# Three dense passes of a graph network: row loads, chunk ends and the graph norm put in a fixed order

## The chip, the cores and the metric

The kernel runs on one core of a Trainium2 chip. The metric is the device time in microseconds (us) of one execution: the median of the kernel before is 2076.03 us over 15 runs (2070.28 to 2085.3). A core has five engines that run at the same time, each with its own queue of instructions: PE (TensorE, products), DVE (VectorE), ACT (ScalarE), POOL (GpSimd) and SP (SyncE, which here only issues DMAs). "PEld" is the load of weights into PE, listed apart.

## What is computed

Four layers over a graph of 6250 nodes with 128 features and 206,250 edges (100,000 pairs in both directions and one loop for each node). Each layer starts with a layer norm and a relu, and is added to its input. Cut to what matters for the change:

```python
# layer 1: mean over neighbours, then a norm over all nodes (one graph)
agg = segment_sum(h[src], dst) / max(deg, 1)
f = gelu(agg @ Wl.T + bl + h @ Wr.T)
out = f - mean_scale * f.mean(0)
x = x + out / sqrt((out * out).mean(0) + EPS) * gn_weight + gn_bias + h
# layer 2: mean over the "cliques" that a node points to (dst clipped to 3124)
x = x + (segment_sum(x_clique[clique], src) / max(count, 1)) @ W.T + b
# layer 3: a gated unit on the sum of messages
hh = relu(layernorm(x)) @ W_in.T + b_in
agg = segment_sum((hh @ W_msg)[src], dst)
r, z = sigmoid(...), sigmoid(...)          # of agg @ W_ih.T and hh @ W_hh.T
n = tanh(i_n + r * h_n)
x = x + ((1 - z) * n + z * hh) @ W_out.T + b_out
```

The sums over edges are taken as products with a matrix of counts: `cnt[s, d]` is the number of edges from node s to node d.

## The kernel before

Nodes are handled in blocks of 128: 49 blocks (`NB`). The first part of the program (to about 1130 us of the profiled execution) goes through the edges in strips, builds the count matrix with one-hot products, writes it to memory (`cnt_d`), writes its transpose for the first 25 blocks (`cntT_d`), and does layer 0 and the products of layer 1 that need no neighbours. It leaves in memory `h_d` (the input of layer 1's sum), `f_d` (the part of layer 1 without neighbours) and `u_d` (the running x). Most strips stand in `with tc.manual_schedule()`: there every engine issues its instructions in the order of the source. Elsewhere a scheduler of the compiler picks the order on each engine.

What follows are three dense passes, written as one generator, `dense` (L889). A pass goes through 13 chunks of destination blocks (`CHUNKS`: twelve of four blocks and, as the seventh, one of a single block), and for each chunk through all source blocks in steps:

- Passes 1 and 3 (`by_node`): 49 source blocks, 7 a step, so 7 steps a chunk. A step's rows are 896 KB, loaded by SP from `cnt_d` (L899).
- Pass 2: 25 blocks of cliques, 5 a step, so 5 steps a chunk. A step's rows are 640 KB from `cntT_d` (L904).

A step loads its rows into the tile `ring` (three buffers), casts them from bf16 to a 32-bit format, a part on DVE into `some` (L910; in pass 1 L917, which also sums the counts) and a part on ACT into `others` (L911, L920), two buffers each, and runs two products for each source block into `acc` (L922): the features are split into two parts (`halves`, L581 and L582) so that single-pass products keep their precision. That makes 14 products a step in passes 1 and 3, 10 in pass 2.

When a chunk's last step is done, its end is worked off: ACT copies `acc` to `wa` (L998, L1049, L1093), and then

- in pass 1: a product with `wl`, DVE adds (L1004), gelu on ACT (L1008), and POOL sums over nodes into `f_sum` (L981);
- after pass 1 the graph norm: a product sums over partitions (L990), DVE subtracts the centre from all blocks (L1031, 13 instructions), ACT squares (L1033), POOL sums, and from these comes `gain` (L1037 to L1040);
- in pass 2: a product with `wc` (L1053), the load of x from `u_d` (SP, L1056), POOL adds (L1057), DVE multiplies and adds (L1058 to L1064), a layer norm (`norm`: statistics on DVE, L555; four relus on ACT, L569), POOL adds `b_out` to x (L1070), the store to `x_d` (SP, L1071), transposes (L1074), a product with `W_in` (L1078), one with `W_msg` (L1082), and the split into the parts that pass 3 uses;
- in pass 3: the gates (L1098 to L1101), L1105 to L1116, a product with `W_out` (L1120), the load of x from `x_d` (SP, L1122), a DVE add (L1124) and the store to the output (SP, L1126).

All these loads and stores go through SP's one queue. In the source of the kernel before a chunk's end stands whole behind its last step, and the scheduler decides where its instructions fall among the steps of the following chunk. Before pass 1 the source loads all of `h_d` and splits it, and after the first chunk it loads `f_d`, the weights (on ACT's queue, L507 and L514), the inverse degrees and all of `x_clique`.

Of the kernel before, what the change touches and what calls it, by code (L numbers as in the profile page):

```python
# [9 lines left out]
F32 = mybir.dt.float32  # L10
I32 = mybir.dt.int32
BF16 = mybir.dt.bfloat16
# [474 lines left out]
def fast(ctx: ExitStack, tc: tile.TileContext, a: dict, out: bass.AP, flag: bass.AP):  # L487
# [62 lines left out]
    def norm(xs, hs, nb):  # L550
# [3 lines left out]
        for j in range(nb):  # L554
            nc.vector.bn_stats(stats[:, j, :], xs[:, j, :])  # L555
            nc.vector.bn_aggr(mv[:, j, :], stats[:, j, :])
        std = small.tile([P, CB], F32, name="f_std")
# [332 lines left out]
    def dense(parts, by_node, seen=None):  # L890

        last, step, dve = (NB, KB, 4) if by_node else (NQB, KQ, 3)
        for c, (g, nb) in enumerate(CHUNKS):
            w = nb * P
            acc = psum.tile([P, CB * P], F32, name="acc", bufs=2)
            for q in range(0, last, step):
                if by_node:
                    t = ring.tile([P, CB, KB, P], BF16, name="ring")
                    nc.sync.dma_start(t[:, :nb].rearrange("p b k n -> p b (k n)"),  # L899
                                      cnt_d[c, :, :nb, q * P : (q + KB) * P])  # L900
                    t = t[:, :nb].rearrange("p b k n -> p k b n")
                else:
                    t = ring.tile([P, KQ, CB, P], BF16, name="ring")
                    nc.sync.dma_start(t[:, :, :nb].rearrange("p k b n -> p k (b n)"),  # L904
                                      cntT_d[:, q : q + KQ, g * P : g * P + w])
                    t = t[:, :, :nb]
                some = wide.tile([P, 4, CB, P], F32R, name="some")
                others = wide.tile([P, 3, CB, P], F32R, name="others")
                if seen is None:
                    nc.vector.tensor_copy(some[:, :dve, :nb], t[:, :dve])  # L910
                    nc.scalar.copy(others[:, : step - dve, :nb], t[:, dve:])  # L911
                for i in range(step):
                    rhs = some[:, i, :nb] if i < dve else others[:, i - dve, :nb]
                    if seen is not None:
                        total = seen[:, c, q + i : q + i + 1]
                        if i < dve:
                            nc.vector.tensor_scalar(rhs, t[:, i], 1.0, None, op0=ALU.mult,  # L917
                                                    op1=ALU.add, accum_out=total)
                        else:
                            nc.scalar.activation(rhs, t[:, i], AF.Copy, accum_out=total)  # L920
                    for j in range(2):
                        nc.tensor.matmul(acc[:, :w], parts[:, q + i, j, :], rhs,  # L922
                                         start=q + i + j == 0, stop=q + i + j == last)
            yield g, nb, acc


    h_parts = late.tile([P, NB, 2, D], F32R, name="parts")
    fh = late.tile([P, NPAD], F32, name="fh")
    f = fh.rearrange("p (b f) -> p b f", f=D)
    for i, (g, nb) in enumerate(GROUPS):  # L930
        nc.sync.dma_start(f[:, g : g + nb, :], rows(h_d, g, nb))
        halves(nc.vector, [h_parts[:, g : g + nb, i, :] for i in range(2)], f[:, g : g + nb, :])
    deg2 = late.tile([P, NCH, NB], F32, name="deg2")
    layer1 = dense(h_parts, True, deg2)
    first = next(layer1)

    for g, nb in GROUPS:
        nc.sync.dma_start(f[:, g : g + nb, :], rows(f_d, g, nb))
    wl, wc, w_in = (weights(late, n) for n in ("WlT", "WcT", "W_inT"))
    w_msg, w_out = (weights(late, n) for n in ("W_msg", "W_outT"))  # L940
    w_ih, w_hh = weights(late, "W_ihT", D, 3 * D), weights(late, "W_hhT", D, 3 * D)
    b_in = weights(late, "b_in", D, 1)
    b_ih, b_hh = weights(late, "b_ih", D, 3), weights(late, "b_hh", D, 3)
    b_rz = late.tile([P, 2], F32, name="f_b_rz")
    nc.vector.tensor_add(b_rz, b_ih[:, :2], b_hh[:, :2])

    mean_scale, gn_weight, gn_bias, bc, b_out = (
        row_everywhere(late, n, a[n]) for n in ("mean_scale", "gn_weight", "gn_bias", "bc", "b_out"))
    b_res = late.tile([P, D], F32, name="f_b_res")
    nc.vector.tensor_add(b_res, gn_bias, bc)  # L950

    inv1 = late.tile([P, NS * SB], F32, name="inv1")
    with nc.allow_non_contiguous_dma(reason="one number for each node, once"):
        nc.sync.dma_start(inv1, deg_d.rearrange("s p w -> (s p w)").rearrange("(b p) -> p b", p=P))
    nc.vector.tensor_scalar(inv1, inv1, 1.0, None, op0=ALU.max)
    nc.vector.reciprocal(inv1, inv1)

    q_parts = late.tile([P, NQB, 2, D], F32R, name="q_parts")  # L960
    for g in range(0, NQB, GB):
        nb = min(GB, NQB - g)
        xq = work.tile([P, GB, D], F32, name="xq")
        n = min(NQ - g * P, nb * P)
        if n < nb * P:
            nc.sync.dma_start(xq[:, nb - 1, :], a["x_clique"][NQ - 1 :, :].to_broadcast([P, D]))
        if n >= P:
            nc.sync.dma_start(xq[:, : n // P, :], rows(a["x_clique"], g, n // P))
        if n % P:
            nc.sync.dma_start(xq[: n % P, nb - 1, :], a["x_clique"][NQ - n % P :, :])  # L970
        halves(nc.gpsimd, [q_parts[:, g : g + nb, i, :] for i in range(2)], xq[:, :nb, :])
    last_row = late.tile([P, 1], F32, name="last_row")
    with nc.allow_non_contiguous_dma(reason="one row, once"):
        nc.sync.dma_start(last_row, a["x_clique"][NQ - 1 :, :].rearrange("o f -> f o"))

# [16 lines left out]

    f_sum = late.tile([P, CB, D], F32, name="f_sum")
    nc.gpsimd.memset(f_sum, 0.0)
    for g, nb, acc in chain((first,), layer1):
        w = nb * P
        agg = work.tile([P, CB * P], F32, name="wa")
        nc.scalar.copy(agg[:, :w], acc[:, :w])  # L998
        pa = psum.tile([P, CB * D], F32, name="pA")
        for j in range(nb):  # L1000
            s = slice(j * D, (j + 1) * D)
            nc.tensor.matmul(pa[:, s], agg[:, s], wl, start=True, stop=True)
        for j in range(nb):
            nc.vector.scalar_tensor_tensor(f[:, g + j, :], pa[:, j * D : (j + 1) * D],  # L1004
                                           inv1[:, g + j : g + j + 1], f[:, g + j, :],
                                           op0=ALU.mult, op1=ALU.add)
        fg = flat(f[:, g : g + nb, :])
        nc.scalar.activation(fg, fg, AF.Gelu)  # L1008
        over_nodes(f_sum, f[:, g : g + nb, :], g, nb)
    p_sum = over_all(f_sum)  # L1010
    center = late.tile([P, D], F32, name="center")
    nc.vector.scalar_tensor_tensor(center, p_sum, 1.0 / N, mean_scale, op0=ALU.mult, op1=ALU.mult)
    last_rows = late.tile([P, P], F32, name="last_rows")
    nc.vector.tensor_copy(last_rows, last_row.to_broadcast([P, P]))
    p_last = psum.tile([P, D], F32, name="pS")
    nc.tensor.matmul(p_last, last_rows, wc, start=True, stop=True)
    last_out = late.tile([P, D], F32, name="last_out")
    nc.scalar.copy(last_out, p_last)
    inv2 = late.tile([P, NB], F32, name="inv2")
    by_source = deg2.rearrange("p d s -> p s d")  # L1020
    nc.vector.tensor_reduce(inv2, by_source, axis=mybir.AxisListType.X, op=ALU.add)
    nc.vector.tensor_scalar(inv2, inv2, 1.0, None, op0=ALU.max)
    nc.vector.reciprocal(inv2, inv2)
    to_last = late.tile([P, NB], F32, name="to_last")
    nc.vector.tensor_reduce(to_last, by_source[:, :, -(-NQB // CB) :], axis=mybir.AxisListType.X, op=ALU.add)
    nc.vector.tensor_mul(to_last, to_last, inv2)

    sq_sum = late.tile([P, CB, D], F32, name="f_sum")
    nc.gpsimd.memset(sq_sum, 0.0)
    for g, nb in GROUPS:  # L1030
        nc.vector.tensor_sub(f[:, g : g + nb, :], f[:, g : g + nb, :], bcast(center, nb))  # L1031
        sq = work.tile([P, GB, D], F32, name="wb")
        nc.scalar.activation(sq[:, :nb, :], f[:, g : g + nb, :], AF.Square)  # L1033
        over_nodes(sq_sum, sq, g, nb)
    p_sq = over_all(sq_sum)
# [9 lines left out]
    for g, nb, acc in dense(q_parts, False):  # L1045
# [22 lines left out]
        for _ in norm(xg, h, nb):  # L1068
            pass
# [120 lines left out]
```

## Time and profile before

| What | us |
|---|---|
| Median of 15 runs | 2076.03 |
| The profiled execution, its own time | 2085.92 |
| Its span, from the first to the last instruction | 2083.9 |
| First product of pass 1 | 1137.1 |
| `wa` copies of pass 1, first, second, last | 1171.5, 1213.7, 1463.0 |
| `wa` copies of pass 2, first and last | 1498.6, 1699.2 |
| `wa` copies of pass 3, first and last | 1725.2, 2068.7 |

The page of the profile gives PE as busy for 90% of the span, DVE 66%, ACT 56% and POOL 22%; the mean granted clock of PE is 0.966 of full speed. The busy share of PE is a mean over stages, so the stages are looked at one by one: the views used below are the busy time of each engine in a window of time, the timeline (start, length, engine, line, operation, tiles, and in brackets how long the engine was idle before and who released it), the waits of an engine (who waited for whom, us in total, times, longest), and the chain of work that ended last. A time such as 1961.05 is in us from the start of the span.

### The profile page before, as it was taken

How to read it: one execution, taken by the hardware profiler on the slowest of the kernel's cores; microseconds unless marked ns; L12 is line 12 of the kernel's file. 1: busy time of each engine (PE TensorE's matmuls, PEld its weight loads, DVE VectorE, ACT ScalarE, POOL GpSimd, SP SyncE). 2: the span in 40 equal slices, each digit the busy share in tenths (PEclk: the TensorE clock that was granted, in tenths of full speed). 3: DMA queues.
4: the chain of work that ended last, by engine and by line, in shares of the span. 5: the costliest groups of instructions: out<-in, count | busy, mean ns of one | idle time of the engine just before them, and what ended most of it. 6: DMA issues, size and time to landing. Idle time of an engine off the chain costs nothing. (4 is left out here: it accounts for less than half of the span.)

```text
span 2083.9 us, 60004 instructions
## 1 busy us (share of the span) xinstructions
PE 1885.4 (90%) x25624; PEld 1539.7 (74%) x25624; DVE 1385.0 (66%) x2957; ACT 1174.7 (56%) x2717; POOL 462.5 (22%) x377
## 2 busy tenths in 40 slices
PE   1699999999999999999997599999699899999998
PEld 0677888888888788888876488888567677778775
DVE  5777787777777777777763587687765564433443
ACT  2866666666666666666661366566454554443443
POOL 3124333343234333343221200000421110000000
PEclk9799999999999999999998799999898999997999
DMA  2466777667867677677635998788476777766773
GB/s 59 125 150 185 178 196 181 182 178 192 187 161 191 182 195 178 181 179 192 165 84 187 245 295 259 232 285 271 123 235 186 224 248 238 237 192 220 237 237 125
DMA packets 423783, 406.29 MB, mean 195 GB/s; under 512 B 191216, under 2 KB 414307, under 8 KB 417235
## 3 DMA queue, kind: packets, MB, share of 16 engines
q1 hardware_dynamic: 414883, 394.35, 66.5%
q0 software_dynamic: 5600, 6.56, 1.2%
q8 instruction: 203, 3.33, 0.7%
q10 hardware_dynamic: 3024, 1.45, 0.4%
q14 instruction: 73, 0.60, 0.1%
HBM read 227.26 MB, written 134.89 MB: 174 GB/s over the span
## 5 line engine op out<-in xcount | busy, mean ns | idle before, releaser
L741 ACT CAST cnt<-pK 128x392 bf16<-128x392 f32 x784 | 405.7, 518 | 303.8 <-PE pK L736 256.1
L766 PE MATMUL pL<-edge_w,h 128*128 128x256 f32 (+1 forms) x2450 | 564.2, 381 | 0.3 <-ACT agg L770 0.3
L766 PEld LDWEIGHTS pL<-edge_w,h 128*128 128x128 f32 x2450 | 447.1, 192 | 56.0 <-ACT agg L770 0.5
L736 PEld LDWEIGHTS <-s_hot 64*128 64x128 bf16 x18816 | 361.8, 96 | 151.6 <-issue 111.7
L736 PE MATMUL pK<-k_hot,s_hot 64*128 64x49 bf16 (+1 forms) x18816 | 404.2, 194 | 68.0 <-ACT edge_w L741 24.4
L741 ACT COPY edge_w<-pK 128x392 f32<-128x392 f32 x784 | 414.5, 529 | 0.0
L922 PE MATMUL acc<-some,parts 128*128 128x512 f32 (+1 forms) x1456 | 374.0, 399 | 32.1 <-DVE some L917 22.0
L922 PEld LDWEIGHTS acc<-some,parts 128*128 128x128 f32 x1456 | 273.7, 196 | 97.2 <-DVE some L917 27.4
L911 ACT CAST others<-ring 128x1536 fp32r<-128x1536 bf16 (+3 forms) x156 | 192.4, 1233 | 203.4 <-PE acc L922 143.8
L715 DVE TENSOR_TENSOR s_hot<-iota,keys 128x2048 bf16<-128x2048 bf16 x196 | 239.1, 1220 | 89.6 <-ACT keys L697 55.1
L910 DVE CAST some<-ring 128x2048 fp32r<-128x2048 bf16 (+3 forms) x156 | 167.2, 1072 | 181.5 <-PE acc L922 171.6
L922 PE MATMUL acc<-others,parts 128*128 128x512 f32 (+1 forms) x1092 | 279.0, 390 | 0.0
L718 DVE TENSOR_TENSOR k_hot<-k_hot,by_edge 128x2352 bf16<-128x2352 bf16 x196 | 272.4, 1390 | 8.0
L917 DVE TENSOR_SCALAR_CACHE_REDUCE some<-ring 128x512 fp32r<-128x512 bf16 (+1 forms) x364 | 216.1, 651 | 66.7 <-DMA ring<-cnt_d 31.8
L922 PEld LDWEIGHTS acc<-others,parts 128*128 128x128 f32 x1092 | 204.5, 194 | 41.7 <-issue 0.5
L920 ACT ACTIVATE others<-ring 128x512 fp32r<-128x512 bf16 (+1 forms) x273 | 162.3, 597 | 112.9 <-issue 47.0
L625 POOL DMA_INDIRECT dst<-in_dst,off_i x50 | 82.4, 1649 | 403.8 <-DVE off_i L659 219.9
L922 PE MATMUL acc<-some,q_parts 128*128 128x512 f32 (+1 forms) x390 | 113.4, 418 | 31.2 <-DVE some L910 31.2
L717 DVE TENSOR_TENSOR k_hot<-iota,keys 128x784 bf16<-128x784 bf16 x196 | 113.5, 579 | 0.0
L922 PEld LDWEIGHTS acc<-some,q_parts 128*128 128x128 f32 x390 | 73.0, 201 | 51.9 <-DVE some L910 36.2
L625 POOL DMA_INDIRECT line<-in_dst,at_i x25 | 40.7, 1627 | 221.3 <-DVE at_i L638 218.7
L922 PE MATMUL acc<-others,q_parts 128*128 128x512 f32 (+1 forms) x260 | 80.3, 419 | 0.0
(158 smaller groups left out, 1571.2 us busy)
## 6 DMA issues: line engine op xcount, KB each, us to landing
ring<-cnt_d SPq DMA_DIRECT2D x168, 896.0 KB
cnt_d<-cnt SPq DMA_DIRECT2D x49, 1568.0 KB
cntT_d<-tt SPq DMA_DIRECT2D x175, 224.0 KB
ring<-cntT_d SPq DMA_DIRECT2D x60, 640.0 KB
ring<-cnt_d SPq DMA_DIRECT2D x14, 224.0 KB
xs<-in_x SPq DMA_DIRECT2D x12, 256.0 KB
xs<-in_x SPq DMA_DIRECT2D x24, 128.0 KB
u_d<-xs SPq DMA_DIRECT2D x24, 128.0 KB
```

The source lines that it names most:

```text
L625: nc.gpsimd.indirect_dma_start(out=t, out_offset=None, in_=col[name], in_offset=bass.IndirectOffsetOnAxis(ap=idx, axis=0))
L715: nc.vector.tensor_tensor(s_hot, count_up(P), at(0, P), op=ALU.is_equal)
L717: nc.vector.tensor_tensor(k_hot[:, :, 0], count_up(NB), at(1, NB), op=ALU.is_equal)
L718: nc.vector.tensor_tensor(k_hot[:, :, 1:], k_hot[:, :, :1].to_broadcast([P, tq, 3, NB, TI]), parts.to_broadcast([P, tq, 3, NB, TI]), op=AL ...
L736: nc.tensor.matmul(pk[:, h, to], s_hot[r, u, :, t], rhs, start=j == 0, stop=True, skip_group_check=True)
L741: nc.scalar.copy(m.rearrange("p b (i h) -> p b i h", h=WN), by_block[:, i])
L766: nc.tensor.matmul(pl[:, :w], h0[:, s, :], edge_w[:, s, :w], start=s == 0, stop=s == NB - 1)
L910: nc.vector.tensor_copy(some[:, :dve, :nb], t[:, :dve])
L911: nc.scalar.copy(others[:, : step - dve, :nb], t[:, dve:])
L917: nc.vector.tensor_scalar(rhs, t[:, i], 1.0, None, op0=ALU.mult, op1=ALU.add, accum_out=total)
L920: nc.scalar.activation(rhs, t[:, i], AF.Copy, accum_out=total)
L922: nc.tensor.matmul(acc[:, :w], parts[:, q + i, j, :], rhs, start=q + i + j == 0, stop=q + i + j == last)
```

## The change

The three passes and the graph norm are put in one `with tc.manual_schedule()`, and the source itself now gives the order. `dense` loads and casts a step's rows (`bring`) one step ahead of its products, and yields after each step. A chunk's end is a generator too, cut by `yield` into pieces; after each step `between` moves every end that is running by one piece, and lets at most three run at once:

```python
        for n, (c, g, nb, q) in enumerate(steps):
            now = ready
            if n + 1 < len(steps):
                ready = bring(*steps[n + 1])
            if q == 0:
                acc = psum.tile([P, CB * P], F32, name="acc", bufs=2)
            for i in range(step):
                for j in range(2):
                    nc.tensor.matmul(acc[:, : nb * P], parts[:, q + i, j, :], now[i],
                                     start=q + i + j == 0, stop=q + i + j == last)
            yield (g, nb, acc) if q + step == last else None

    running, waiting = [], []

    def between(free=True):

        running[:] = [work for work in running if next(work, work) is not work]
        if free and waiting and len(running) < 3:
            running.append(waiting.pop(0))

    def run(layer, end, chores=()):

        chores = iter(chores)
        for done in layer:
            between()
            for chore in next(chores, ()):
                chore()
            if done:
                work = end(*done)
                next(work)
                waiting.append(work)
```

The first piece of an end is the copy of `acc`. Pass 1's end has two more, pass 2's eleven, pass 3's five. These are the pieces of pass 2's and pass 3's ends that hold the stores:

```python
        for _ in steps:
            pass
        nc.gpsimd.tensor_tensor(xg, xg, bcast(b_out, nb), op=ALU.add)
        nc.sync.dma_start(rows(x_d, g, nb), xg)
        yield
...
        yield
        po = psum.tile([P, CB * D], F32, name="pA", bufs=2)
        for j in range(nb):
            o = po[:, j * D : (j + 1) * D]
            nc.tensor.matmul(o, new[:, j * P : (j + 1) * P], w_out, start=True, stop=True)
        xg = flat(x[:, :nb, :])
        nc.vector.tensor_add(xg, xg, po[:, :w])
        if g + nb < NB:
            nc.sync.dma_start(rows(out, g, nb), x[:, :nb, :])
```

(The loop over `steps` is the rest of `norm`: DVE's reciprocal and shift, and the four relus.) The graph norm is a generator of thirteen pieces that runs beside the first thirteen steps of pass 2, two groups of four blocks to a piece; until it is through, pass 2's ends wait:

```python
        for i, (g, nb) in enumerate(GROUPS):
            nc.vector.tensor_sub(f[:, g : g + nb, :], f[:, g : g + nb, :], bcast(center, nb))
            sq = work.tile([P, GB, D], F32, name="wb", bufs=3)
            nc.scalar.activation(sq[:, :nb, :], f[:, g : g + nb, :], AF.Square)
            over_nodes(sq_sum, sq, g, nb)
            if i % 2:
                yield
...
        layer2 = dense(q_parts, False)
        next(layer2)
        normed = running[-1]
        for done in layer2:
            between(normed not in running)
            if done:
                work_2 = end2(*done)
                next(work_2)
                waiting.append(work_2)
        layer3 = dense(m_parts, True)
        next(layer3)

        def rest():
            while running or waiting:
                between()

        while waiting or len(running) > 2:
            between()
        run(layer3, end3, [[]] * 4 + [[rest]])
        rest()
```

The other edits: `h_d` is loaded and split group by group within the first chunk of pass 1, as its steps come to need it; the loads of `f_d`, `x_clique`, the weights and the rows of biases become "chores" put behind single steps of pass 1, a few to a chunk, and all go through SP; `m_parts` takes the place of `h_parts` in the same tile, `sq_sum` gets a tile of its own; `wa` has five buffers instead of two, `x` and `wb` three instead of two, `xq` one instead of two, and in PSUM `pA` has two and there is a new tile `pM`; the layer norm's statistics can be cut in two (a `yield 2` in `norm`). The products and the numbers that are computed stay the same.

## The prediction

> **What bounds the kernel now.** I read the busy time by stage first, cut where the ACT copies of a finished chunk (`wa<-acc`, lines 998, 1049, 1093) begin. The columns are the window, its length, the busy us (and instructions) of PE, PEld, DVE, ACT and POOL, the granted clock, the DMA share and GB/s:
>
> ```profile
> 1171.50:1213.60 42.10, 27.73 (x107) 20.57 (x108) 22.09 (x71) 18.10 (x51) 9.37 (x11) 0.80 0.92 255
> 1213.60:1463.00 249.40, 247.79 (x1162) 205.00 (x1161) 194.02 (x656) 153.59 (x479) 13.40 (x11) 0.99 0.82 265
> 1463.00:1498.60 35.60, 18.38 (x77) 14.28 (x77) 26.35 (x25) 15.70 (x24) 22.67 (x16) 0.72 0.36 107
> 1498.60:1699.20 200.60, 183.15 (x850) 140.99 (x850) 123.00 (x326) 104.96 (x166) 32.47 (x23) 0.96 0.70 213
> 1699.20:2068.70 369.50, 368.04 (x1531) 279.14 (x1530) 156.60 (x185) 159.68 (x148) 1.31 (x1) 0.97 0.69 224
> ```
>
> The dense passes run from 1137 (first `acc` matmul) to the end. Pass 1 is the first two rows: its second chunk takes 42.1 us, the others 23.4, PE full. Row 3 is the graph norm: PE idle for 17.2 us and on a low clock. Row 4 is pass 2: 17.4 us idle. Row 5 is pass 3: 1.5 us idle in 369.5. So what this change can win lies in pass 1's second chunk, the graph norm and pass 2; pass 3 has only its one-block chunk to win, and everything to lose.
>
> Second, the waits of SP, the queue that issues every row load of the passes:
>
> ```profile
> SPq L1126 <- DVE x L1124: 83.6, 12, 9.2
> ...
> SPq L1071 <- POOL x L1070: 37.9, 13, 5.1
> ```
>
> SP stands still before each store of a chunk until its data is ready; whatever is queued behind the store waits as well. Third, the timeline of pass 3 around one such store:
>
> ```profile
> 1961.05 1.13 PE L1120 MATMUL pA<-f_W_outT,wd 128*128 128x128 f32 x8
> ...
> 1962.22 0.69 DVE L1124 TENSOR_TENSOR x<-x,pA 128x512 f32<-128x512 f32 x1 [0.18 <-PE pA L1120]
> ...
> 1962.93 0.38 SPq L1126 DMA_DIRECT2D out<-x  x1
> 1964.23 0.54 SPq L899 DMA_DIRECT2D ring<-cnt_d  x1
> ```
>
> The output products end, DVE adds, SP stores at once, and the next row load waits only for its ring slot: the ACT cast before it ended at 1964.21. In this kernel the load follows as soon as a slot is free, so the store costs nothing. Fourth, what a row load takes when SP issues it late, at the start of pass 3 (two issues in one entry, at 1689.57 and 1690.50):
>
> ```profile
> 1689.57 1.47 SPq L899 DMA_DIRECT2D ring<-cnt_d  x2
> ...
> 1694.52 1.23 DVE L910 CAST some<-ring 128x2048 fp32r<-128x2048 bf16 x1 [2.31 <-DMA ring<-cnt_d]
> ...
> 1698.71 1.23 DVE L910 CAST some<-ring 128x2048 fp32r<-128x2048 bf16 x1 [2.96 <-DMA ring<-cnt_d]
> ```
>
> 896 KB land 4.95 us after issue, and the second load 3.3 us (4.19 less the 0.93 between issues) behind that.
>
> **The change, part by part.** In the changed source the order on SP is: rows of step n+1, then the DMAs of the end-pieces put after step n, then rows of step n+2. `E` is the end of step n's 14 matmuls.
>
> *Output stores in pass 3.* The last piece of a chunk's end (four products, add, store) is put after step 5 of the next chunk. The products run from E to E+1.05 (eight records, 1.06 at 1961 by the chain), the add ends 0.2+0.69 later, the store is issued at E+1.95 and takes 0.38: the rows of step n+2 go out at E+2.35. They land at E+7.3, the cast takes 1.23 (row above), PE can start step n+2 at E+8.6. Meanwhile it has only step n+1 to run, 14 matmuls in 3.2 us (86 in 19.70 us by the chain): done at E+4.25. Stall 4.3 us. I add 0.4, since the rows after these land 3.3 us later and a step is 3.2: 4.7. Eleven stores have rows behind them (the last one's steps are all loaded), one of them beside the short steps of the one-block chunk (1.6 more): 53 us. Bounds: a landing of 6.7 us (issue 1185.37, cast 1192.09) gives 72; a landing that is hidden gives 0. I take 4.95, since nothing else then fills the queue.
>
> *Stores of x_d in pass 2.* The piece with the relus comes after step n. ACT does the casts of step n+1 first, then:
>
> ```profile
> 1673.46 1.65 ACT L569 ACTIVATE wb<-x,f_shift,f_rstd 128x128 f32<-128x128 f32 x4 [0.44 <-DVE f_shift L565]
> 1675.18 1.28 POOL L1070 TENSOR_TENSOR x<-x,f_b_out 128x512 f32<-128x512 f32 x1 [8.07 <-ACT wb L569]
> ...
> 1676.48 0.36 SPq L1071 DMA_DIRECT2D x_d<-x  x1
> ```
>
> From relu to store is 3.0 us. ACT's casts (1.05) can't start before step n-1 frees `others`; counted from that, the store is at 1.25+3.0 = 4.3, the rows of n+2 at 4.75. 640 KB scaled from 896 KB (1.4 fixed, as 256 KB in 2.3 of the chain's `x_d<-x` leave after 0.9 at 285 GB/s, and 2.5 for the bytes) land 4.0 later, the cast takes 0.96: 9.7. PE has steps n and n+1 (10 matmuls, 2.29 each) and about 1.0 of pieces: 5.6 to 6.0. Stall 3.7, 4.7 if DVE is behind; I take 4.2. Counting the yields, the graph norm holds the ends back for 13 steps; then stores fall after steps 20, 21, 22, 31, 32, 37, 42, 47, 52, 57, 62. A store that follows another by one step finds no cover: 5.8. So 8 x 4.2 + 3 x 5.8 = 51 us, bounds 0 and 70.
>
> *What goes in pass 2:* the 17.4 us idle and the low clock (0.96 of 200.6 us, 8 us), 25 in all, if the pieces, a step apart, no longer make PE wait. Net +26.
>
> *Graph norm between steps.* Gone: 17.2 us idle and 4 us at half clock. New: seven steps with two subtractions each. In the trace 13 of them take 18.25 us on DVE beside POOL, 1.40 each, so 2 x 1.40 + 0.96 of cast = 3.76 a step against 2.29 of matmuls: 10.3 lost. Net -11, bounds -21 and 0.
>
> *Pass 1.* The second chunk goes from 42.1 to about 26: the loads of f, x_clique and the weights no longer stand in front of its rows. The first stays: h and rows, 9.6 MB at 258 to 285 GB/s, are 34 to 37 us, as now (34.5). The moved loads, 5.7 MB, come back in the steady chunks, at 265 GB/s now and 285 then, near the 316 GB/s of the fastest slice. Net -16, bounds -19 and 0. Its DVE waits (products, four adds of 0.34, then casts) fit in a step; if not, 0.2 a chunk.
>
> *From pass 2 to pass 3.* The last end is flushed after step 4 with nothing beside it (relu, transposes, copy, W_in, copy, W_msg, split: 8.2 us to PE's release, 2.4 of it PE work): 6. One pass 2 store holds rows of pass 3: 4. Products moved over: 3. The one-block chunk takes 28.1 us now, with a 6.3 us chain of gates and half clock; 6.5 of end products and the 14.0 it takes in pass 1 make 20.5, and the chunk after it gains 1.5: 9 back. Net +4.
>
> Sum: -16 - 11 + 26 + 53 + 4 = **+56**. The profiled execution took 2085.92 (span 2083.9), 9.9 above the median 2076.03 of 15; I add the difference to the median: **2132**.
>
> **Rules weighed.** The Trainium skill, "DMA: Bandwidth & Descriptors", section "Anatomy of one DMA — SWDGE (gpsimd) path", says that waits are served on the issuing sequencer before dispatch, which speaks against this order as SP's rows above do. Its fit for that path, 2.0 us plus bytes over 436 GB/s, would make the landing 4.1, an estimate, and the sum some 9 us smaller; the row's 4.95 decides. "TensorE: Matmul & The Clock Gate", Part 1, has the clock halve after an idle window of about 3.4 us, which my stalls exceed; by it each could cost up to 1.7 us more, an estimate.
>
> **Rivals.**
> 1. *The rows arrive in time* (SP's order is not the source's, or waits resolve earlier than I count), so both store terms vanish: -16 - 11 - 25 + 0 + 0 = -52, and rival DVE waits give some back: about **2028**. It decides where a store is issued 3 us before E. For it: three ring slots, and SP waits 83.6 us now without harm. Against: the strips already run in a fixed order, and there SP waits 164.5 us for its stores of `cnt` with transposes behind them.
> 2. *Stalls half as long*, since pieces of other chunks cover them: 56 - 52 = +4, **2080**.
> 3. *The clock falls after stalls.* After 2.3 us idle at 1671.8 the slice to 1680 has 0.91, 1.8 us lost; after 6.2 us near 1877 the next slice has 0.50. 22 stalls x 1.8 = 40 more: **2172**.
>
> **Numbers.** Forecast 0.62 (2105 to 2160), rival 3 0.13 (to 2190), rival 2 0.07 (2060 to 2105), rival 1 0.18. The range, 2060 to 2190, leaves out rival 1. 0.2% (4 us) is about what a measurement here can tell from no change: faster 0.22 (rival 1 and half of 2), same 0.03, slower 0.75.
>
> **What would show it.** Right: in pass 3 one PE gap of 4 to 5 us per chunk, before step 0, with the cast waiting for a row load that SP issued right after `out<-x`; chunks of some 33.6 us where they were 28.9; the same after `x_d<-x` in pass 2; no 42 us chunk in pass 1; no 14.7 us gap in the graph norm. Wrong: pass 3 still at 28.9 us per chunk, or casts that wait for something other than rows.

## The result, and the profile after

The changed kernel takes 2173.96 us (median of 9 runs, 2167.82 to 2176.8), the kernel before 2076.96 (47 runs): a ratio of 1.0461, 95% interval 1.0445 to 1.0477. It is slower by 97 us, where the forecast said 56 (2132, range 2060 to 2190). The profiled execution has a span of 2167.4 us and a mean granted clock of 0.957, where the one of before has 2083.9 and 0.966.

The first view of the changed kernel is again the busy time by stage, cut at the `wa<-acc` copies (now L1048). The rows are the second chunk of pass 1, pass 2 with the graph norm beside it, and pass 3; columns as before (window, length, busy us and instructions of PE, PEld, DVE, ACT and POOL, granted clock, DMA share, GB/s):

```profile
1169.90:1193.20 23.30, 23.30 (x107) 19.27 (x106) 19.08 (x63) 15.86 (x45) 1.29 (x1) 1.00 0.94 322
1442.50:1712.80 270.30, 209.27 (x903) 165.09 (x901) 157.75 (x349) 113.29 (x180) 54.91 (x39) 0.87 0.55 171
1712.80:2150.10 437.30, 381.19 (x1552) 287.60 (x1552) 158.15 (x191) 164.72 (x159) 2.56 (x2) 0.94 0.55 191
```

The second chunk of pass 1 takes 23.3 us where it took 42.1, and PE is never idle in it. Pass 2 takes 270.3 (before, 35.6 + 200.6 = 236.2) and pass 3 takes 437.3 (before, 369.5); in both PE now waits, at a lower clock and with the DMA engines half busy. By stage the change is -20.9 (pass 1: from the first product at 1137.5 to 1442.5), +34.1, +67.8 and +2.1 (what follows the last copy), together 83, the difference of the two spans.

The waits of SP, before the stores of the output and of `x_d`:

```profile
SPq L1201 <- DVE x L1199: 154.3, 12, 13.5
SPq L1138 <- POOL x L1137: 153.3, 13, 17.1
```

SP stands 308 us before these stores, where it stood 121.5 before the change. What stands behind shows in the timeline of a chunk of pass 3 (an entry that covers several issues, such as `x5`, gives the start of the first):

```profile
2001.80 2.00 PE L936 MATMUL acc<-some,parts 128*128 128x512 f32 x8
...
2006.10 0.69 DVE L1199 TENSOR_TENSOR x<-x,pA 128x512 f32<-128x512 f32 x1 [4.24 <-PE pA L1197]
2006.82 0.40 SPq L1201 DMA_DIRECT2D out<-x  x1
2007.30 9.74 SPq L902 DMA_DIRECT2D ring<-cnt_d  x5
...
2012.52 1.23 DVE L913 CAST some<-ring 128x2048 fp32r<-128x2048 bf16 x1 [5.74 <-DMA ring<-cnt_d]
...
2013.81 3.59 PE L936 MATMUL acc<-some,parts 128*128 128x512 f32 x8 [4.52 <-DVE some L913]
```

This is the forecast's sequence, item by item: DVE's addition behind the output products, SP's store as soon as it is done, the next rows 0.48 us later, the cast 5.2 after that, and PE idle for 4.52. One thing is new: the eight products behind the gap take 3.59 us, and eight such products take 2.00 us in a step without a gap (the first line). The same in pass 2, after the store of `x_d`:

```profile
1679.33 1.56 PE L936 MATMUL acc<-some,q_parts 128*128 128x512 f32 x6
...
1680.57 0.36 SPq L1138 DMA_DIRECT2D x_d<-x  x1
...
1681.09 5.92 SPq L907 DMA_DIRECT2D ring<-cntT_d  x4
...
1685.58 0.96 DVE L913 CAST some<-ring 128x1536 fp32r<-128x1536 bf16 x1 [6.76 <-DMA ring<-cntT_d]
...
1686.59 2.93 PE L936 MATMUL acc<-some,q_parts 128*128 128x512 f32 x6 [4.34 <-DVE some L913]
```

PE is idle for 4.34 us, and then six products take 2.93 us where six took 1.56 in the step before (the first line).

### The profile page after: what moved, and what is told of

Same layout as the page of the kernel before. It is cut to its first block, busy times and chain, and to the rows that moved or that the text cites. A ratio compares the mean times of both kernels' runs of the same rounds, so it can differ in the third digit from the quotient of the medians.

```text
span 2167.4 us, 60053 instructions
## 1 busy us (share of the span) xinstructions
PE 1902.9 (88%) x25624; PEld 1557.8 (72%) x25624; DVE 1390.4 (64%) x2957; ACT 1171.8 (54%) x2717; POOL 459.3 (21%) x377
## 5 line engine op out<-in xcount | busy, mean ns | idle before, releaser
L936 PE MATMUL acc<-some,parts 128*128 128x512 f32 (+1 forms) x1456 | 384.8, 409 | 71.3 <-DVE some L913 54.2
L936 PE MATMUL acc<-some,q_parts 128*128 128x512 f32 (+1 forms) x390 | 117.8, 443 | 60.2 <-DVE some L913 60.2
L936 PEld LDWEIGHTS acc<-some,q_parts 128*128 128x128 f32 x390 | 77.8, 214 | 84.7 <-DVE some L913 66.7
L627 POOL DMA_INDIRECT src<-in_src,off_i x50 | 75.9, 1517 | 15.4 <-issue 14.9
```

What stands on the lines that cost most here:

```text
L627: nc.gpsimd.indirect_dma_start(out=t, out_offset=None, in_=col[name], in_offset=bass.IndirectOffsetOnAxis(ap=idx, axis=0))
L936: nc.tensor.matmul(acc[:, : nb * P], parts[:, q + i, j, :], now[i], start=q + i + j == 0, stop=q + i + j == last)
```

## The experiments

The theory: row loads stand behind a store that waits on SP's queue; they land too late for the one step of cover that they have; and after the gap the products run slow. Its rivals: the pieces of the ends on PE, ACT and DVE cost the time, whichever queue the stores are on (A); the bytes of the stores beside the rows do (B); the clock is low for other reasons (C).

The runs are compared from the first product of the passes to the end of the span, "the passes", since the part ahead of them, which no edit touches, is not always equally long: it ends at 1136 to 1143 us in most profiles, but at 1188 to 1195 in e1 to e3 and e6, beside which the kernel before took 2135.68 us. The lengths, in us, cut at the same copies, are each read from one profiled execution; two executions of the changed kernel differ by 7 us in the passes, two of the kernel with both stores on POOL by 1:

| Kernel | time | ratio to before, 95% interval | pass 1 | pass 2 | pass 3 | end | the passes |
|---|---|---|---|---|---|---|---|
| before | 2076.96 | | 325.9 | 236.2 | 369.5 | 15.2 | 946.8 |
| changed | 2173.96 | 1.0461 (1.0445 to 1.0477) | 305.0 | 270.3 | 437.4 | 17.3 | 1030 |
| after_again | 2176.39 | 1.0470 (1.0436 to 1.0503) | 307.7 | 268.4 | 444.1 | 17.3 | 1037 |
| e1_out_2later | 2166.39 | 1.0147 (1.0098 to 1.0196) | 307.7 | 272.6 | 369.5 | 18.0 | 968 |
| e2_xd_2later | 2163.52 | 1.0135 (1.0080 to 1.0189) | 306.3 | 205.7 | 438.1 | 17.1 | 967 |
| e3_both_2later | 2087.83 | 0.9781 (0.9741 to 0.9821) | 306.6 | 209.1 | 364.8 | 18.1 | 899 |
| e6_pool_stores | 2086.75 | 0.9779 (0.9738 to 0.9819) | 307.9 | 204.7 | 359.3 | 20.1 | 892 |
| e4_both_1later | 2083.53 | 1.0017 (1.0001 to 1.0033) | 306.7 | 222.8 | 388.4 | 18.0 | 936 |
| e5_rows_3ahead | 2056.34 | 0.9883 (0.9857 to 0.9909) | 317.1 | 224.2 | 362.0 | 18.0 | 921 |
| e7_fill_gap | 2163.77 | 1.0401 (1.0373 to 1.0429) | 307.5 | 269.4 | 423.0 | 19.3 | 1019 |
| e6_again | 2029.34 | 0.9738 (0.9708 to 0.9769) | 306.5 | 204.2 | 359.2 | 21.4 | 891 |
| e8_pool_onegroup | 2028.89 | 0.9731 (0.9707 to 0.9755) | 307.8 | 197.7 | 359.2 | 21.5 | 886 |
| e9_act_out | 2027.93 | 0.9729 (0.9696 to 0.9761) | 307.4 | 203.2 | 359.5 | 17.8 | 888 |
| e10_pool_ahead3_onegroup | 2046.71 | 0.9813 (0.9787 to 0.9838) | 315.8 | 205.8 | 360.5 | 21.3 | 903 |

e1 to e3 and e6 were measured together, then after_again, e4, e5 and e7, both groups on a chip that the record numbers 15, and the last four together on chip 9. Why the part ahead took some 50 us more in the first group is not known. Every edit is one of the changed kernel, except where another is named.

**Each store two steps later, alone and together.** e1 moves the output store, e2 the store of `x_d`, e3 both.

```diff
         nc.vector.tensor_add(xg, xg, po[:, :w])
+        yield
+        yield
         if g + nb < NB:
             nc.sync.dma_start(rows(out, g, nb), x[:, :nb, :])
```

```diff
         nc.gpsimd.tensor_tensor(xg, xg, bcast(b_out, nb), op=ALU.add)
-        nc.sync.dma_start(rows(x_d, g, nb), xg)
         yield
...
         yield
+        nc.sync.dma_start(rows(x_d, g, nb), xg)
         ph = psum.tile([P, CB * P], F32, name="pB")
```

> The store of a chunk's output comes two steps later in the source; nothing else changes. Theory (rows stand behind the store on SP's queue, and their landing of some 5 us, the cast and the half clock after the gap are paid once a chunk): two steps later the output is long ready, SP does not wait there, pass 3 goes from 35 us a chunk back to about 29, its 437 us to about 370, passes 1 and 2 stay; about 2110 us, between 2100 and 2120. Rival A (the cost of pass 3 is PE's end pieces and DVE's adds in front of its casts, whichever queue the store is on): no change, 2174. Rival B (it is the store's bytes beside the rows): no change either, the gap only moves two steps.

> The store of x to x_d in pass 2 comes two pieces later in the source (ahead of the W_in product); nothing else changes. Theory (SP's queue): the eleven stalls of pass 2 go, 20.8 us a chunk back to about 16.5, pass 2 from 270 to some 215 us; pass 3 stays at 437; about 2120 us, between 2105 and 2135. Rival A (pieces on PE, ACT and DVE in the program's order): pass 2 stays near 270, 2174. Rival C (the clock, low for other reasons): gaps go but the granted clock of pass 2 stays near 0.87 and half of the gain is missing, about 2147.

> Both stores two steps later. Theory: the gains of the two alone add up, since they lie in different passes: pass 2 about 215 us, pass 3 about 370, some 120 us less than the changed kernel: 2050 us, between 2040 and 2065, and so below the kernel before (2077). Rival A or B: near 2174. If the half clock after gaps was a cost of its own, the mean granted clock rises from 0.957 to 0.97 or more.

The passes fall from 1030 us by 62 with e1, by 63 with e2 and by 131 with e3, near the sum of the two, and each edit changes its own pass alone: e1 takes pass 3 from 437.4 to 369.5 and leaves pass 2, e2 takes pass 2 from 270.3 to 205.7, further than the 215 expected, and leaves pass 3. (The whole times that the expectations give were missed by 38 to 56 us, since they counted on the shorter part ahead of the passes; the stages are what can be compared.) Rivals A and B, which expected no change, are out. Rival C is too: the granted clock of e2's pass 2 is 0.98 where it was 0.87, so it was low because of the gaps.

**The same places, another queue.** e6 leaves the stores where the change put them in the source, and issues them on POOL's queue.

```diff
-        nc.sync.dma_start(rows(x_d, g, nb), xg)
+        nc.gpsimd.dma_start(rows(x_d, g, nb), xg)
...
-            nc.sync.dma_start(rows(out, g, nb), x[:, :nb, :])
+            nc.gpsimd.dma_start(rows(out, g, nb), x[:, :nb, :])
```

> Both stores keep their place in the source but are issued on POOL's queue, so that no row load stands behind them; their bytes and times are the same. Theory (the order on SP's queue): as with both stores later, 2050 us, between 2040 and 2070. Rival B (the store's bytes or its writes beside the rows): as the changed kernel, 2174. Rival A (pieces on the engines): 2174 as well.

> The kernel with both stores on POOL's queue once more, beside the runs of this call: dense passes 892 us as in its first profile, whatever the part ahead of them takes here.

Passes of 892 and 891 us, on two chips: the queue on which the stores wait makes the difference. The same data leave at the same points, and in pass 3 of e6_again PE has no gap of 1 us left. In the timeline of e6_again the store waits on POOL as it did on SP, and the products of the step that was late (the last line) follow without a gap:

```profile
1889.64 1.15 POOL L1201 DMA_DIRECT2D out<-x  x1 [27.94 <-DVE x L1199]
...
1891.67 1.99 PE L936 MATMUL acc<-some,parts 128*128 128x512 f32 x8
```

The Trainium skill, "DMA: Bandwidth & Descriptors", section "Issuing engines are not separate DMA queues", says that issuing on several engines saves no more than the sequencer's time to initiate a DMA, which is usually small. The issue itself is small here too (0.40 us on SP, 1.15 on POOL), and still the move is worth some 138 us, since what it saves is the time that a sequencer stands before the issue.

This kernel also gives the size of the two parts of the cost. Its stages, passes 2 and 3:

```profile
1442.60:1646.80 204.20, 188.62 (x903) 151.09 (x902) 162.51 (x349) 113.15 (x180) 66.53 (x50) 0.97 0.78 230
1646.80:2005.90 359.10, 356.90 (x1552) 273.36 (x1552) 158.06 (x191) 164.70 (x159) 18.22 (x16) 1.00 0.71 231
```

PE has as many instructions as in the changed kernel (903 and 1552), but is busy 20.7 us less in pass 2 and 24.3 less in pass 3. The lengths differ by 66.1 and 78.2. So of the 144 us that the stores cost on SP's queue, 45 are products that ran slower, and 99 are time in which PE stood. (With after_again in place of the first profile it is 149, of which 48 and 101.)

**How much cover is enough.** e4 puts both stores one step later, e5 leaves the stores and issues the rows three steps ahead in the source, casts as they were.

```diff
         nc.gpsimd.tensor_tensor(xg, xg, bcast(b_out, nb), op=ALU.add)
+        yield
         nc.sync.dma_start(rows(x_d, g, nb), xg)
-        yield
         pt = psum.tile([P, CB * P], F32, name="pT")
...
         nc.vector.tensor_add(xg, xg, po[:, :w])
+        yield
         if g + nb < NB:
```

```diff
+            m = steps.index((c, g, nb, q))
+            while len(fetched) < min(m + 3, len(steps)):
+                fetched.append(fetch_rows(*steps[len(fetched)]))
+            t = fetched[m]
```

> Both stores one step (one piece) later instead of two. Theory: in pass 3 the output is added at 2.0 us after the end of step n and SP reaches the store only after the rows of step n+2, whose slot comes free with the casts of step n+1; the store then waits for nothing, so one step is as good as two: dense passes 890 to 905 us, some 130 less than the changed kernel. In pass 2 relu and POOL's addition end 3.0 us after the casts of step n+1, a step is 2.3: 0.7 to 2 us of wait are left in front of rows with a step of cover, so at most 10 us more than with two steps. Rival (what counts is the distance of the store from the end of a chunk, or the rows' own bandwidth): a good part of the stalls stays, dense passes above 940 us.

> The stores stay where the change put them; the row loads stand three steps ahead in the source instead of one (same ring of three, casts as they were), so the store of step n is followed by rows that are needed two steps later than before. Theory (a late issue costs only what the cover of rows already landed does not hide): the landing of 5 us lies beside two steps of 3.2 (pass 3) or 2.3 us (pass 2); pass 3 near 29 us a chunk, pass 2 near 15 to 16; dense passes 890 to 915 us. Rival (the store's place between the products is what costs, not the rows' cover): as the changed kernel, 1030 us.

e4 missed its expectation: 936 us, 37 above e3. The expectation was reckoned wrongly, and the forecast's own sum shows where. The store of e4 still waits for DVE's addition 1.95 us after step n, since the ring's slot for the rows before it comes free earlier than I had assumed; the rows of n+3 stand behind it and can be cast by 8.6 us after step n, as before. But PE now has two steps to run, not one: 1.05 + 2 x 3.2 = 7.45. That leaves 1.1 us. The timeline of e4 shows it:

```profile
1996.62 0.38 SPq L1202 DMA_DIRECT2D out<-x  x1
1997.10 7.27 SPq L902 DMA_DIRECT2D ring<-cnt_d  x4
...
2002.37 1.23 DVE L913 CAST some<-ring 128x2048 fp32r<-128x2048 bf16 x1 [4.63 <-PE acc L936]
...
2003.65 2.12 PE L936 MATMUL acc<-some,parts 128*128 128x512 f32 x8 [1.35 <-DVE some L913]
```

Issue to cast 5.27 us, and a gap of 1.35. A chunk takes 30.1 us, 1.6 more than the 28.5 of e3 and e6. And behind a gap of 1.35 us the eight products take 2.12 us: no slow clock. e5 has pass 3 at 28.5 us a chunk without touching a store, as expected; its passes are 6 us above the expected range because the first chunk of pass 1 takes 42.9 us, where the runs with rows one step ahead have 32.4 to 34.6 (why was not tried), and pass 2 keeps a part of its waits (224.2 against 204.2).

**The slow products by themselves.** e7 puts 14 products that nobody reads into the gap of pass 3.

```diff
             nc.sync.dma_start(out[(NB - 1) * P :, :], x[:NR, nb - 1, :])
+        if g + nb < NB:
+            yield
+            for _ in range(14):
...
+                nc.tensor.matmul(spare, m_parts[:, 0, 0, :],
+                                 m_parts[:, 0:2].rearrange("p b i d -> p (b i d)"),
+                                 start=True, stop=True)
```

> The changed kernel itself, unaltered, beside the runs of this call: ratio to the kernel before 1.046, and from the first product of the dense passes to the end 1030 us, as in the first profile, whatever the part ahead of the passes takes on this chip.

> The changed kernel with 14 products of 128x512 more per chunk in pass 3, whose result nobody reads, put behind the products of the step after the output store, where PE waits for rows: 14 x 0.229 = 3.2 us of a gap of 4.5. They add work and no wait. Theory with the half clock as a cost of its own (eight products take 3.59 instead of 2.00 us after the gap): the clock stays up, 11 x 1.3 to 1.6 us come back, pass 3 some 14 to 20 us shorter than the 437 of the changed kernel, in spite of the work. Rival (the low clock after the gap costs nothing, the rows would be late anyway): pass 3 unchanged or up to 10 us longer.

Pass 3 takes 423.0 us, 14 less than in the first profile of the changed kernel and 21 less than in the second, on the same chip as e7. More work on PE, and it ends sooner. The step after the gap in e7:

```profile
2041.67 3.35 PE L1210 MATMUL pM<-parts 128*128 128x512 f32 x14
...
2046.24 2.12 PE L936 MATMUL acc<-some,parts 128*128 128x512 f32 x8 [1.22 <-DVE some L913]
```

1.22 us of idle are left of 4.5, and the eight products take 2.12 us. A chunk takes 33.3 us: the 33.6 of the forecast, whose gap alone was in the sum. The low clock is a cost of its own. after_again came to 1037 us instead of 1030; two profiles of one kernel differ by 7 in pass 3.

**Which work may stand behind a waiting store, and the graph norm.** e9 has the store of `x_d` on POOL, as e6, and the output store on ACT, in front of ACT's casts. e8 is e6 with one group of the graph norm to a step instead of two, and e10 is e8 with the rows of e5 (the two edits shown there and here).

```diff
-            nc.sync.dma_start(rows(out, g, nb), x[:, :nb, :])
+            nc.scalar.dma_start(rows(out, g, nb), x[:, :nb, :])
```

```diff
             over_nodes(sq_sum, sq, g, nb)
-            if i % 2:
-                yield
+            yield
```

> The store of x_d on POOL's queue, the output store on ACT's, in their places. Theory (a wait costs what stands behind it and is needed within the wait): ACT then stands some 2 us after step n before the casts of step n+2, whose rows have landed and which PE needs 4.2 us after step n; the cast takes 1.23, so nothing is late: dense passes 890 to 900 us, as on POOL's queue. Rival (any in-order queue with work of the products behind a waiting store costs a gap): pass 3 keeps gaps of 1 to 3 us a chunk, dense passes above 905.

> Both stores on POOL's queue, and in the graph norm one group of subtraction and square per step instead of two. Theory (the graph norm's loss is DVE's time in steps that are too full): the second chunk of pass 2, 19.9 us with DVE busy throughout, falls to 15.5 to 17.5, spread over 13 steps; the ends start six steps later, which the passes can make up; dense passes 886 to 890 us, 2 to 6 less than with two groups. Rival (the delayed ends pile up at the change to pass 3, whose first chunk takes 32.4 us now): that chunk grows by 3 us or more and the sum is 892 or above.

> Both stores on POOL's queue, rows three steps ahead in the source, one group of the graph norm per step. Theory: with the stores off SP's queue only the loads of u_d and x_d stand between the rows there, which the ring covers; rows further ahead bring 0 to 3 us in pass 1 and nothing behind it: dense passes 884 to 890 us. Rival (more rows in flight hold up the loads that the ends wait for): 892 or above.

e9 is as fast as e6 (888 us). Its timeline at an output store:

```profile
1893.71 0.38 ACTq L1201 DMA_DIRECT2D out<-x  x1
1894.20 1.48 ACT L914 CAST others<-ring 128x1536 fp32r<-128x1536 bf16 x1 [3.79 <-DVE x L1199]
...
1897.84 1.53 PE L936 MATMUL acc<-others,parts 128*128 128x512 f32 x6
```

ACT stands 3.79 us, issues the store and then casts; the cast ends at 1895.68, 2.2 us before the products that read it, and PE has no gap. So a waiting store is not dear as such; it costs what is late behind it.

e8 takes 197.7 us in pass 2, 6.5 less than e6_again, and pass 3's first chunk stays at 32.4, so the rival's pile-up does not come there. The second chunk of pass 2 falls from 19.9 us to 13.4, below the 15.5 to 17.5 expected, while some later chunks grow (the sixth from 13.7 to 19.8, the eighth from 14.6 to 22.9). In the medians e8 and e6_again differ by 0.45 us, which their intervals can't tell apart: the 5 us of the profiles are a reading of two executions and no verdict. DVE's subtractions are a part of it: instructions of line L1082 in e6_again and in e8, with shortest, median and longest in ns:

```profile
L1082 DVE TENSOR_TENSOR fh<-fh,center x13: 678/1761/1791, 1453.1 to 1476.4; 128x512 f32<-128x512 f32 x12, 128x128 f32<-128x128 f32 x1
```

```profile
L1082 DVE TENSOR_TENSOR fh<-fh,center x13: 677/685/1786, 1454.4 to 1484.8; 128x512 f32<-128x512 f32 x12, 128x128 f32<-128x128 f32 x1
```

The same subtraction of 128x512 takes 0.68 or 1.78 us. Of the twelve, seven take the longer time in e6_again and four in e8: 15.4 us in all against 12.6. In both timelines every long one starts while one of POOL's additions is running, and no short one does. These 2.8 us are less than half of the 6.5; that the rest comes from steps that are less full fits the expectation and is not shown by itself. e10 missed: 903 us, where its rival had 892 or above, though not for a reason that was shown. Its first chunk of pass 1 takes 42.4 us, as e5's, and pass 2 is 8 us longer than e8's: with the stores off SP's queue, rows further ahead bring nothing here. Why the first chunk and pass 2 grew was not tried.

## Why the prediction was right in kind and too small

**Stores and rows (right in mechanism).** The forecast's stall was 4.3 us in pass 3, in a sequence of eight steps; the trace shows 4.52 with the same steps. Rows take 5.2 us from issue to cast in pass 3 (4.95 in the forecast) and 4.5 in pass 2 (4.0). The forecast's "some 9 us smaller" for a landing of 4.1 us counts the stalls of pass 3 alone. In sum it had 53 + 51 us of stalls and 4 at the change of passes, 108; the runs show 99: 54 in pass 3 (78.2 - 24.3) and 45 in pass 2 (66.1 - 20.7). The three stores in successive steps (20, 21 and 22), of which I had the late ones at 5.8, lie in the chunk of 40.9 us, from 1507.55 to 1548.41, with gaps of 6.32, 3.56 and 5.02: 14.9 us where the sum had 15.8, but with the longest gap first and not last.

**The clock after the stall (the step that failed).** The forecast took the price of a stall as the time in which PE stands, and left the low clock to rival 3, at 22 x 1.8 = 40 us and a chance of 0.13. The runs show 45 us of slower products, 2.0 a stall, and e7 shows that they go when the gap is filled. Rival 3's 2172 is close to the measured 2174, partly by luck: its sum is +96 and the spans differ by 83. The evidence in the forecast, beside the stages with 14.4 and 17.2 us of idle and clocks of 0.80 and 0.72, was a row: behind 2.31 us of idle at 1671.82 the clock fell (0.66 up to 1676). Another was misread: near 1877 PE stands idle for 1.40 us, not 6.2, and the granted clock is 0.50 from 1878 to 1900, while PE runs products of 128 columns. And the trace of before has rows on the other side, which the forecast did not weigh: behind 2.72 and 2.45 us of idle (1636.71 and 1654.34) six products took 1.67 us, at full clock. What was wrong was to hold a second term of the same stalls for a separate case, when the forecast's stalls of 4.3 us were longer than all of these. The Trainium skill, "TensorE: Matmul & The Clock Gate", Part 1, has the clock halve after an idle window of about 3.4 us. The forecast's estimate by it, up to 1.7 us a stall, is near the 2.0 measured. The runs agree for most of the gaps: 4.52 us of idle, eight products in 3.59; 1.35 or 1.22 us of idle, 2.12. They don't show one threshold. The first line is from the long chunk of pass 2 in the changed kernel, where behind 5.02 us six products took 2.93; the second is from e4:

```profile
1531.09 1.67 PE L936 MATMUL acc<-some,q_parts 128*128 128x512 f32 x6 [3.56 <-DVE some L913]
```

```profile
1886.31 3.44 PE L936 MATMUL acc<-some,parts 128*128 128x512 f32 x8 [2.40 <-DVE some L913]
```

So 3.56 us of idle cost nothing in the products behind it, and 2.40 us cost 1.4. What decides between the two the runs don't show.

**Pass 1 (right, 2 to 5 too small).** -20.9 for -16, and -18.2 in after_again. The second chunk came to 23.3 instead of 26; the DMA engines move 322 GB/s in it. The moved loads cost no time in the steady chunks, as the sum had it: these take 23.34 us (before, 23.37), and from the third chunk on the engines move 283 GB/s, where I had reckoned with 285. The other 2 us of the -20.9 lie in the first chunk (32.4 for 34.4), which after_again does not show (34.5).

**Graph norm and idle time of pass 2 (near).** Without the stalls pass 2 takes 204.2 us (e6_again), 32 less than before; the sum had 25 + 11 = 36.

**Pass 3 without stalls (too high by 10).** 359.2 us (e6_again) against 369.5; the sum had +6 + 3 - 9 = 0. The chunk that covers the flush is 6.4 longer than before (32.4 for 26.0), the one-block chunk 10.6 shorter (17.5 for 28.1), the one after it 2.3, and nine of the other ten 0.4 each.

**Spans and medians.** The terms sum to -21 - 32 - 10 + 99 + 45 + 2 = 83, which is the difference of the spans. The 27 us by which this exceeds the forecast's 56 are the 45 of the clock less 18 of smaller misses in the other terms, most of them downwards, so the forecast came nearer than its missing term. The other 14 of the 97 us are the choice of executions: the one profiled of before (2085.92) lay 9.0 above the median of the 47 runs, the one of the changed kernel (2169.25) 4.7 below its own.

Of the rivals, 1 (the rows arrive in time, 2028) described what the kernel becomes when the stores leave SP's queue: e6_again takes 2029.34. The closeness of the two is partly luck, since the kernel before took 2082.49 beside it; as differences they are -48 and -53. The distance from there to the changed kernel is what the order of one queue cost.

## What to carry to other kernels

When a source fixes the order of instructions, a queue that issues both the loads that feed the machine and stores that wait for results will serve the loads at the pace of the results; put stores on a queue where nothing is due behind them, or behind so many steps that their data are long ready. The test is arithmetic: release of the store, plus issue, landing and conversion of what stands behind it, against the work that the bottleneck still has; in e4 it gives a gap of 1.1 us where 1.35 were measured, and in e9 it gives none, as measured. And price a stall of the TensorE twice, once for the time it stands and once for the clock after it, whenever the trace shows the clock falling after an idle time of that length.

## What the runs showed of the hardware

- The cost of the clock after a gap does not grow evenly with it: 1.22 and 1.35 us of idle cost nothing that can be seen (eight products of 128x512 in 2.12 us; 2.09 behind the output products without a gap), 4.52 us cost 1.6 in the next eight products alone. Between these the length of the gap does not settle it: 2.40 us cost 1.4 in e4, 3.56 us cost nothing in the changed kernel.
- Fourteen products whose results are thrown away made pass 3 14 to 21 us shorter.
- DVE's subtraction of 128x512 takes 0.68 us, or 1.78 where it starts while one of POOL's additions is running (seven of twelve in e6_again, four in e8); so dividing that work over more steps shortened the work itself, from 15.4 us to 12.6. That the overlap is the cause is read from the timeline and was not tried by itself.
